# Gathering expert rows in four parts for VectorE's transposes, and a new order of the first products

## The chip, the cores and the metric

The kernel runs on one core of one Trainium2 chip. The metric is device time in microseconds, of which the median over several executions is given. TensorE is called PE here (its weight loads PEld), VectorE DVE, ScalarE ACT, GpSimd POOL and the engine that issues most transfers SP.

## What is computed

One image of 256 channels and 48 x 48 = 2304 tokens passes through two layers, all in float32. Layer 0 normalises groups of channels, and adds attention over all tokens and four heads. Layer 1 adds an attention through 64 slices, and then a mixture of experts, which is the stage that the change is mostly about:

```python
x = x + _L0_conv_ref(_gn(x), ...)          # _gn: mean and variance over 32 groups of 8 channels
t = _to_tokens(x)                          # 2304 tokens of 256
t = t + _L1_attn_ref(_ln_t(t), ...)
...
gate_logits = xf @ Wg + bg                 # xf = _ln_t(t), 8 experts
top_w, top_i = jax.lax.top_k(gate_logits, 2)
top_w = jax.nn.softmax(top_w, axis=-1)
for e in range(8):
    h = gelu(xf @ W1[e] + b1[e])           # 256 -> 1024
    out = out + w_dense[:, e:e+1] * (h @ W2[e] + b2[e])
t = t + out
```

## The kernel before

**Front.** SP loads x in four pieces and then the weights Wq, Wk, Wv, Wo. `transposed` (L249) turns a 256 x 256 weight by four PE transposes into a PSUM tile `pw` of a ring of two, which ACT copies out. DVE reduces x to mean and variance of each channel (`mv`). A product of PE with `gmat` spreads the means over groups (`pg`, L275), DVE forms `dm`, a second product spreads the variances (`pg2`, L286), and DVE and POOL make `rstd` of it. Then DVE normalises x into `xn` (kept in `t_sb`), block by block of 512 tokens, and PE multiplies by Wq and Wk (L312, L316) and later Wv. A transpose of `brow` gives the biases as columns. `busy_first` (L263) adds a product whose result nobody reads. The engines' instructions are in most places kept in program order by `InOrder`, so that their line in the profile is that of the helper, L60.

**Gating** (from L1035). After the attention and the slices, DVE finds two experts for each token and a place for each of the 4608 choices in slots of 128 rows, each slot of one expert. There are 43 slots at most (`NSL`); 36 (`SURE`) are in use at least, and three more (`near`) are prepared. PE's products end in `pw`: for each row of a slot its token and weight. DVE turns that into `slot_t` (token, int32) and `slot_w`. Rows that no token fills point to one of 128 empty rows behind the 2304. `busy(n, spin)` runs n idle products of 256 columns. The normalised tokens lie in DRAM as `tn_d`, and the sum is kept in DRAM as `t_d`.

**Expert tiles** (from L1296). For each slot s:

- `rows` (L1226): one indirect DMA, issued by POOL, gathers 128 rows of 1 KB from `tn_d` into `xs`, a ring of two tiles.
- `load_w1` (L1234): SP loads the expert's W1, 1 MB, into a ring of two. W2 of all experts is already in SBUF.
- `turn` (L1241): PE transposes the two halves of `xs` into PSUM (`pt`), DVE copies them to `xT`.
- `first` (L1250): 16 products into `ph`, and ACT's gelu into `hid`.
- `second` (L1268): 8 products into `py` and DVE's bias and weight, into `y`. Behind the third product a function `meanwhile` is called, in which the turn of another slot stands.
- `scatter` (L1288): an indirect DMA of POOL adds the rows of `y` to `t_d`.

Each "product" in float32 is two matmul instructions in the profile. The main loop (L1348) is written so that iteration s issues `first(s)`, then the gather of slot s+2 and its W1 load, then `second(s-1)` with the turn of slot s+1 in it, then `scatter(s-1)`. Indirect DMAs are kept in written order on POOL (`issued`), so the gather of s+2 stands behind the scatter of s-2 and before that of s-1. A scatter waits until the one before has landed.

At s == 4, `judge` tests the ranges of the first attention's sums; it has a transpose `pm`. The rows of the last slot, 35, are not scattered: PE adds them at the end by a product with `here`, a 0/1 matrix of 128 rows by 2304 tokens. It is made from an iota of POOL (at s == 6) and comparisons of DVE with `held` (L1366, L1369). At the end `t_d` is read back, transposed by PE and written out.

Of the kernel before, what the change touches and what calls it, by code (L numbers as in the profile page):

```python
# [9 lines left out]
FP = mybir.dt.float32  # L10
AF = mybir.ActivationFunctionType
ALU = mybir.AluOpType
AX = mybir.AxisListType
PSUM = bass.MemoryType.PSUM

P = 128
C = 256
NT = 2304
NTT = NT // P
# [17 lines left out]
NSL = (2 * NT - E) // P + E  # L37
# [9 lines left out]
def bc(ap, shape):  # L47

    return ap.unsqueeze(2).to_broadcast(shape)
# [16 lines left out]
def layers(  # L66
# [69 lines left out]
    )  # L136

    stats = const.tile([P, NTT, 2], FP, name="stats")
    rstd_t = const.tile([P, NTT], FP, name="rstd_t")
# [81 lines left out]
    def rsqrt(dst, var, eps, n):  # L221

        ve = small.tile([P, n], FP, name="ve", tag="ve")
        dve.tensor_scalar(ve, var, eps, None, ALU.add)
        nc.gpsimd.tensor_tensor(dst, ve, mhalf[:, 0:n], ALU.pow)
# [18 lines left out]
    with proj, tc.tile_pool(name="ps_pj", bufs=5, space=PSUM) as ps_pj, tc.tile_pool(  # L244
        name="ps_spun", bufs=1, space=PSUM
    ) as ps_spun, tc.tile_pool(
        name="ps_w", bufs=2, space=PSUM
    ) as ps_w:
        def transposed(dst, raw):  # L249
            pw = ps_w.tile([P, 2, C], FP, name="pw", tag="pw")  # L250
            for ci in range(2):
                for co in range(2):
                    pe.transpose(
                        pw[:, ci, co * P : (co + 1) * P], raw[:, co, ci * P : (ci + 1) * P], ident
                    )
            nc.scalar.copy(dst, pw)
            return dst

        WqT = transposed(pj.tile([P, 2, C], FP, name="WqT"), raws["Wq"])
        WkT = transposed(pj.tile([P, 2, C], FP, name="WkT"), raws["Wk"])  # L260
        spun = ps_spun.tile([P, 256], FP, name="spun")

        def busy_first(n):  # L263
            for _ in range(n):
                pe.matmul(spun, ident, raws["Wq"][:, 0, :], start=True, stop=True)


# [6 lines left out]
        gm = gmat.rearrange("p a b -> p (a b)")  # L274
        pg = ps_w.tile([P, 512], FP, name="pw", tag="pw")  # L275
        pe.matmul(pg[:, 0:2], gm, mv[:, :, 0], start=True, stop=True)
        busy_first(1)
        dm = pj.tile([P, 2], FP, name="dm")
        dve.tensor_sub(dm, mv[:, :, 0], pg[:, 0:2])
        for c in range(2):  # L280
# [3 lines left out]
        mean = pj.tile([P, 2], FP, name="mean")  # L284
        dve.tensor_copy(mean, pg[:, 0:2])
        pg2 = ps_w.tile([P, 512], FP, name="pw", tag="pw")  # L286
        pe.matmul(pg2[:, 0:2], gm, dm, start=True, stop=True)
        rstd = pj.tile([P, 2], FP, name="rstd")
        rsqrt(rstd, pg2[:, 0:2], 1e-5, 2)
        xn = t_flat[:, 0 : 2 * NT].rearrange("p (c n) -> p c n", c=2)  # L290
        pb = ps_w.tile([P, 512], FP, name="pw", tag="pw")
        pe.transpose(pb[:, 0:78], brow, ident[0:78, 0:78])
        dve.tensor_copy(bcol, pb[:, 0:78])
        bq8 = pj.tile([P, 2], FP, name="bq8")
        dve.tensor_scalar(bq8, bcol[:, B_Q : B_Q + 2], 0.125, None, ALU.mult)
        WvT = transposed(pj.tile([P, 2, C], FP, name="WvT"), raws["Wv"])
        transposed(WoT, raws["Wo"])


        for bi, (t0, tn) in enumerate(TBLOCKS):  # L300
# [34 lines left out]
            if bi == 0:  # L335
                later_constants()

        def slice_weights():
# [71 lines left out]
    def busy(n, bank):  # L410

        for _ in range(n):
            pe.matmul(bank[:, 0:256], ident, Wqkv_sb[:, 0, 0:256], start=True, stop=True)
# [422 lines left out]
    gp = gating.enter_context(tc.tile_pool(name="gate", bufs=1))  # L836
    norm = gating.enter_context(tc.tile_pool(name="norm", bufs=2))


# [194 lines left out]
    slot_w = route.tile([P, NSL], FP, name="slot_w")  # L1034
    slot_t = route.tile([P, NSL], mybir.dt.int32, name="slot_t")  # L1035
    b1_e = bcol[:, 0 : E * NHC].rearrange("p (e f) -> p e f", e=E)
    b2_e = b2_bc.rearrange("p (e d) -> p e d", e=E)
    with gating, tc.tile_pool(name="onehot", bufs=1) as oh, tc.tile_pool(
# [113 lines left out]
        for n in (3, 6, 6, 3, 6, 6, 3, 3):  # L1152
# [22 lines left out]
            k += n  # L1175
        busy(11, spin)

        empties = gp.tile([P, NSL], FP, name="empties")
        dve.tensor_scalar(empties, pw[:, 0, :], 0.0, spare, ALU.is_equal, ALU.mult)
        dve.scalar_tensor_tensor(empties, pw[:, 0, :], -1.0, empties, ALU.add, ALU.add)  # L1180
        dve.tensor_scalar(slot_t, empties, 0.0, float(NT + P - 1), ALU.max, ALU.min)
        dve.tensor_copy(slot_w, pw[:, 1, :])

    def expert_of(s, engine):
# [6 lines left out]
    with tc.tile_pool(name="ps_h", bufs=1, space=PSUM) as ps_h, tc.tile_pool(  # L1191
# [17 lines left out]
        here = fin.tile([P, NT], FP, name="here")  # L1209
        held = fin.tile([P, 1], FP, name="held")  # L1210
        obs = cycle([fin.tile([P, 2, 512], FP, name=f"ob{k}") for k in range(3)])
# [14 lines left out]
        def rows(s, xs):  # L1226
# [5 lines left out]
            return xs  # L1232

        def load_w1(s, w1):  # L1234
            e = expert_of(s, mybir.EngineType.SP)
            nc.sync.dma_start(
                out=w1, in_=W1[bass.ds(e, 1)].rearrange("e (c p) f -> p (e c) f", p=P)
            )
            return w1

        def turn(xs):  # L1241

            pt = next(ring_pt)
            for c in range(2):
                pe.transpose(pt[:, c, :], xs[:, c * P : (c + 1) * P], ident)
            xT = next(ring_xT)
            dve.tensor_copy(xT, pt)
            return xT

# [50 lines left out]
        for s in range(2):  # L1300
            w1[SURE + s] = load_w1(SURE + s, next(ring_w1))
            xs[s] = rows(s, next(ring_xs))
        used = nc.values_load(
# [12 lines left out]
        def turn_next(s):  # L1316
            if s in xs:
                xT[s] = turn(xs.pop(s))

# [28 lines left out]
        for s in range(SURE):  # L1348
            hid[s] = first(s, xT.pop(s), w1.pop(s))
            if s + 2 < SURE:  # L1350
                xs[s + 2], w1[s + 2] = rows(s + 2, next(ring_xs)), load_w1(s + 2, next(ring_w1))
            if s == 0:
                turn_next(1)
            elif s < SURE - 2:
                scatter(s - 1, second(s - 1, hid.pop(s - 1), lambda: turn_next(s + 1)))
            if SURE - 3 <= s < SURE - 1:

                scatter(s, second(s, hid.pop(s), lambda: turn_next(s + 1) if s == SURE - 2 else None))
            if s == 4 and bad is not None:
                judge()  # L1360
            if s == 6:
                pool.iota(
                    here, pattern=[[1, NT]], base=0, channel_multiplier=0,
                    allow_small_or_imprecise_dtypes=True,
                )
                dve.tensor_copy(held, slot_t[:, SURE - 1 : SURE])  # L1366
            if 8 <= s < 8 + len(TBLOCKS):
                t0, n = TBLOCKS[s - 8]
                dve.tensor_scalar(here[:, t0 : t0 + n], here[:, t0 : t0 + n], held, None, ALU.is_equal)  # L1369

# [95 lines left out]
```

## Time and profile before

| | us |
|---|---|
| median of 3 runs | 1587.24 |
| lowest and highest | 1586.57, 1590.79 |
| the profiled execution | 1588.82 |
| its span, first to last instruction | 1587.1 |
| PE busy in it | 1559.0 (98%) |
| DVE, ACT, POOL busy | 1034.2, 830.7, 192.7 |
| transposes pt of slots' rows on PE | 72 matmuls of 0.273 |
| gathers xs on POOL | 36 of 1.08 |
| scatters on POOL | 38 of 1.58 |

The profile is that of one execution. A group of it is named by line, engine and operation, then output<-inputs, their size, and how often (x). In a timeline each row has its start, its duration, and in brackets how long the engine sat idle before it and who ended that. Matmuls overlap, so the time of one is read from the distance of starts. "issue" is idle time in which the engine waited for nothing that the profile shows.

### The profile page before, as it was taken

How to read it: one execution, taken by the hardware profiler on the slowest of the kernel's cores; microseconds unless marked ns; L12 is line 12 of the kernel's file. 1: busy time of each engine (PE TensorE's matmuls, PEld its weight loads, DVE VectorE, ACT ScalarE, POOL GpSimd, SP SyncE). 2: the span in 40 equal slices, each digit the busy share in tenths (PEclk: the TensorE clock that was granted, in tenths of full speed). 3: DMA queues.
4: the chain of work that ended last, by engine and by line, in shares of the span. 5: the costliest groups of instructions: out<-in, count | busy, mean ns of one | idle time of the engine just before them, and what ended most of it. 6: DMA issues, size and time to landing. Idle time of an engine off the chain costs nothing. (4 is left out here: it accounts for less than half of the span.)

```text
span 1587.1 us, 32093 instructions
## 1 busy us (share of the span) xinstructions
PE 1559.0 (98%) x13117; PEld 776.2 (49%) x13117; DVE 1034.2 (65%) x1291; ACT 830.7 (52%) x1167; POOL 192.7 (12%) x133
## 2 busy tenths in 40 slices
PE   7999999999999999999999999999999999999998
PEld 3633343333333333333333333333334689999996
DVE  6578787787777778878778778787787721111111
ACT  3256565555666556556556566566554533323231
POOL 0001001011010010110101101101010123433331
PEclk9999999999999999999999999999999999999999
DMA  4000000000000000000000000000000956666665
GB/s 136 1 1 1 1 1 3 6 1 1 9 1 1 8 1 2 7 2 2 4 5 2 2 8 1 1 8 1 1 2 28 331 161 193 175 190 174 192 171 161
DMA packets 55981, 79.30 MB, mean 50 GB/s; under 512 B 21471, under 2 KB 42158, under 8 KB 55694
## 3 DMA queue, kind: packets, MB, share of 16 engines
q1 hardware_dynamic: 47826, 66.45, 13.0%
q0 software_dynamic: 7344, 10.10, 3.8%
q8 instruction: 108, 1.77, 0.5%
q10 hardware_dynamic: 652, 0.56, 0.1%
q14 instruction: 51, 0.42, 0.1%
HBM read 62.94 MB, written 12.32 MB: 47 GB/s over the span
## 5 line engine op out<-in xcount | busy, mean ns | idle before, releaser
L60 ACT ACTIVATE p<-s 128x1024 f32<-128x1024 f32 x648 | 663.3, 1024 | 470.4 <-PE s L60 465.2
L60 DVE TENSOR_TENSOR acc<-acc,p 128x1024 f32<-128x1024 f32 x612 | 749.5, 1225 | 243.3 <-ACT p L60 237.5
L60 PE MATMUL av<-p,v_sb 64*64 64x512 f32 x5184 | 675.7, 590 | 3.1 <-ACT p L60 1.9
L60 PE MATMUL s<-q,kk 64*64 64x512 f32 x5184 | 674.7, 589 | 0.5 <-DVE tn L60 0.5
L60 PEld LDWEIGHTS s<-q,kk 64*64 64x64 f32 x5184 | 202.1, 133 | 353.6 <-issue 181.5
L60 PEld LDWEIGHTS av<-p,v_sb 64*64 64x64 f32 x5184 | 195.7, 131 | 358.5 <-ACT p L60 201.6
L60 ACT ACTIVATE hid<-ph,bcol 128x128 f32<-128x128 f32 x312 | 89.5, 368 | 199.9 <-PE ph L60 199.1
L60 POOL PARTITION_ALL_REDUCE total<-both x17 | 71.2, 4186 | 1012.6 <-ACT p L60 893.9
L60 PE MATMUL py<-w_sb,hid 128*128 x624 | 146.9, 379 | 0.0
L60 PEld LDWEIGHTS ph<-xT,w 128*128 128x128 f32 x1248 | 145.3, 192 | 2.7 <-issue 0.8
L60 PE MATMUL ph<-xT,w 128*128 128x128 f32 x1248 | 145.7, 275 | 0.6 <-issue 0.6
L60 DVE COPY xT<-pt 128x256 f32<-128x256 f32 x39 | 16.5, 425 | 161.0 <-PE pt L60 161.0
L60 PEld LDWEIGHTS py<-w_sb,hid 128*128 128x128 f32 x624 | 112.9, 190 | 12.3
L1217 POOL DMA_INDIRECT t_d<-y,slot_t x38 | 60.1, 1581 | 163.2 <-DVE y L60 145.4
L60 DVE TENSOR_TENSOR y<-py,b_bc 128x256 f32<-128x256 f32 x39 | 16.6, 425 | 77.4 <-PE py L60 77.4
L1217 POOL DMA_INDIRECT xs<-tn_d,slot_t x36 | 38.8, 1078 | 15.9 <-issue 10.1
L60 DVE RECIPROCAL rinv<-rinv 128x256 f32<-128x256 f32 x17 | 29.7, 1746 | 0.0
L60 DVE TENSOR_TENSOR acc<-p 128x1024 f32<-128x1024 f32 x18 | 22.1, 1226 | 4.9 <-ACT p L60 3.3
L329 DVE TENSOR_SCALAR q<-pp,bcol 64x512 f32<-64x512 f32 (+1 forms) x30 | 20.8, 694 | 6.7 <-PE pp L312 6.4
L60 DVE TENSOR_REDUCE up<-av 128x512 f32<-128x1024 f32 x17 | 20.8, 1225 | 5.0 <-PE av L60 5.0
L60 POOL TENSOR_TENSOR rstd_t<-ve,mhalf 128x2 f32<-128x2 f32 (+2 forms) x13 | 11.1, 850 | 103.2 <-DVE ve L60 95.7
L60 PE MATMUL spin<-Wqkv_sb,ident 128*128 128x256 f32 x84 | 19.4, 381 | 0.0
(295 smaller groups left out, 590.6 us busy)
## 6 DMA issues: line engine op xcount, KB each, us to landing
w<-in_L_ffn_W_dram SPq DMA_DIRECT2D x39, 1024.0 KB, 5.9
w_sb<-in_L_ffn_W_dram SPq DMA_DIRECT2D x8, 1024.0 KB, 11.8
t_sb<-turned SPq DMA_DIRECT2D x224, 8.0 KB, 1.8
x_sb<-in_x_dram SPq DMA_DIRECT2D x3, 576.0 KB, 4.9
t_d<-t_sb SPq DMA_DIRECT2D x2, 768.0 KB, 10.2
tn_d<-tn SPq DMA_DIRECT2D x2, 768.0 KB, 5.7
t_sb<-t_d SPq DMA_DIRECT2D x3, 512.0 KB, 4.1
out_dram<-ob SPq DMA_DIRECT2D x3, 512.0 KB, 3.0
```

The costliest lines, as they stand in the source:

```text
L60: return self.tc.keep_in_program_order(getattr(self.engine, name)(*args, **kwargs))
L329: nc.vector.tensor_scalar(dst, pq[rows, 0:tn], bcol[rows, B_Q + m : B_Q + m + 1], 0.125, ALU.add, ALU.mult,)
L1217: new = nc.gpsimd.indirect_dma_start(**kwargs)
```

## The change

In the front, the means' product moves ahead of Wk's transposes, and the variances' product and the biases' transpose stand between the first two and the last two of them. The three results get a PSUM bank of their own (`pgb`). `busy_first` goes. Wo's transposes move behind the first block of q and k products.

For 26 of the slots (`in_parts`: s from 2 to 35 but those with s % 4 == 1), the gather is split in four. `part_t` holds for each slot and part k the index of a 256-byte quarter row: partition 32q + s gets quarter q of the token of row 32k + s. So each 32 x 32 block that DVE transposes by itself already lies where its transpose belongs, and two DVE transposes from `xs` to `xT` take the place of PE's two and the copy. `quad` (made by ACT), `quarter`, four products and one DVE step make `part_t` in the gating, and the 11 idle products there become 4 and 5. Channels are now dealt to partitions in pairs (2p + c instead of 128c + p), in W1's load and in both kinds of turn.

For the last slot, `here` is made by DVE alone from `steps` and `held`, which now has a column for each block of 128 tokens; POOL's iota goes.

```diff
+    quarter = const.tile([P, 1], FP, name="quarter")
+    for q in range(4):
+        nc.vector.memset(quarter[q * 32 : (q + 1) * 32, :], float(q))
     stats = const.tile([P, NTT, 2], FP, name="stats")
...
     with proj, tc.tile_pool(name="ps_pj", bufs=5, space=PSUM) as ps_pj, tc.tile_pool(
-        name="ps_spun", bufs=1, space=PSUM
-    ) as ps_spun, tc.tile_pool(
+        name="ps_g", bufs=1, space=PSUM
+    ) as ps_g, tc.tile_pool(
         name="ps_w", bufs=2, space=PSUM
     ) as ps_w:
-        def transposed(dst, raw):
+        def transposed(dst, raw, meanwhile=lambda: None):
             pw = ps_w.tile([P, 2, C], FP, name="pw", tag="pw")
             for ci in range(2):
                 for co in range(2):
                     pe.transpose(
                         pw[:, ci, co * P : (co + 1) * P], raw[:, co, ci * P : (ci + 1) * P], ident
                     )
+                if ci == 0:
+                    meanwhile()
             nc.scalar.copy(dst, pw)
             return dst
         WqT = transposed(pj.tile([P, 2, C], FP, name="WqT"), raws["Wq"])
-        WkT = transposed(pj.tile([P, 2, C], FP, name="WkT"), raws["Wk"])
-        spun = ps_spun.tile([P, 256], FP, name="spun")
-        def busy_first(n):
-            for _ in range(n):
-                pe.matmul(spun, ident, raws["Wq"][:, 0, :], start=True, stop=True)
+        pgb = ps_g.tile([P, 96], FP, name="pgb")
+        pg = pgb[:, 0:4].rearrange("p (a b) -> p a b", a=2)
+        pb = pgb[:, 16:94]
...
         gm = gmat.rearrange("p a b -> p (a b)")
-        pg = ps_w.tile([P, 512], FP, name="pw", tag="pw")
-        pe.matmul(pg[:, 0:2], gm, mv[:, :, 0], start=True, stop=True)
-        busy_first(1)
+        pe.matmul(pg[:, 0, :], gm, mv[:, :, 0], start=True, stop=True)
         dm = pj.tile([P, 2], FP, name="dm")
-        dve.tensor_sub(dm, mv[:, :, 0], pg[:, 0:2])
+        dve.tensor_sub(dm, mv[:, :, 0], pg[:, 0, :])
         for c in range(2):
             dve.scalar_tensor_tensor(
                 dm[:, c : c + 1], dm[:, c : c + 1], dm[:, c : c + 1], mv[:, c, 1:2], ALU.mult, ALU.add
             )
         mean = pj.tile([P, 2], FP, name="mean")
-        dve.tensor_copy(mean, pg[:, 0:2])
-        pg2 = ps_w.tile([P, 512], FP, name="pw", tag="pw")
-        pe.matmul(pg2[:, 0:2], gm, dm, start=True, stop=True)
+        dve.tensor_copy(mean, pg[:, 0, :])
+        def spread():
+            pe.matmul(pg[:, 1, :], gm, dm, start=True, stop=True)
+            pe.transpose(pb, brow, ident[0:78, 0:78])
+        WkT = transposed(pj.tile([P, 2, C], FP, name="WkT"), raws["Wk"], spread)
         rstd = pj.tile([P, 2], FP, name="rstd")
-        rsqrt(rstd, pg2[:, 0:2], 1e-5, 2)
+        rsqrt(rstd, pg[:, 1, :], 1e-5, 2)
         xn = t_flat[:, 0 : 2 * NT].rearrange("p (c n) -> p c n", c=2)
-        pb = ps_w.tile([P, 512], FP, name="pw", tag="pw")
-        pe.transpose(pb[:, 0:78], brow, ident[0:78, 0:78])
-        dve.tensor_copy(bcol, pb[:, 0:78])
+        dve.tensor_copy(bcol, pb)
         bq8 = pj.tile([P, 2], FP, name="bq8")
         dve.tensor_scalar(bq8, bcol[:, B_Q : B_Q + 2], 0.125, None, ALU.mult)
         WvT = transposed(pj.tile([P, 2, C], FP, name="WvT"), raws["Wv"])
-        transposed(WoT, raws["Wo"])
...
                 later_constants()
+                transposed(WoT, raws["Wo"])
...
     norm = gating.enter_context(tc.tile_pool(name="norm", bufs=2))
+    quad = gp.tile([P, 4, 4, 32], FP, name="quad")
+    act.copy(quad, ident.rearrange("p (k s) -> p k s", k=4).unsqueeze(2).to_broadcast([P, 4, 4, 32]))
...
     slot_t = route.tile([P, NSL], mybir.dt.int32, name="slot_t")
+    part_t = route.tile([P, 4, NSL], mybir.dt.int32, name="part_t")
     b1_e = bcol[:, 0 : E * NHC].rearrange("p (e f) -> p e f", e=E)
...
             k += n
-        busy(11, spin)
-        empties = gp.tile([P, NSL], FP, name="empties")
+        busy(4, spin)
+        empties = route.tile([P, NSL], FP, name="empties")
         dve.tensor_scalar(empties, pw[:, 0, :], 0.0, spare, ALU.is_equal, ALU.mult)
         dve.scalar_tensor_tensor(empties, pw[:, 0, :], -1.0, empties, ALU.add, ALU.add)
         dve.tensor_scalar(slot_t, empties, 0.0, float(NT + P - 1), ALU.max, ALU.min)
+        dve.tensor_scalar(empties, empties, 0.0, float(NT + P - 1), ALU.max, ALU.min)
         dve.tensor_copy(slot_w, pw[:, 1, :])
+        pq = ps_lg.tile([P, 4, NSL], FP, name="pq")
+        for k in range(4):
+            pe.matmul(
+                pq[:, k, :], quad[:, k, :, :].rearrange("p q s -> p (q s)"), empties, start=True, stop=True,
+            )
+        dve.tensor_scalar(part_t, pq, 4.0, quarter, ALU.mult, ALU.add)
+        busy(5, spin)
...
         here = fin.tile([P, NT], FP, name="here")
-        held = fin.tile([P, 1], FP, name="held")
+        held = fin.tile([P, NTT], FP, name="held")
         obs = cycle([fin.tile([P, 2, 512], FP, name=f"ob{k}") for k in range(3)])
...
+        def in_parts(s):
+            return 2 <= s < SURE and s % 4 != 1
+        def parts(s, xs):
+            if not in_parts(s):
+                return rows(s, xs)
+            for k in range(4):
+                indirect(
+                    out=xs[:, k * 64 : (k + 1) * 64], out_offset=None,
+                    in_=tn_d.rearrange("t (q d) -> (t q) d", q=4),
+                    in_offset=bass.IndirectOffsetOnAxis(ap=part_t[:, k, s : s + 1], axis=0),
+                    bounds_check=4 * (NT + P) - 1, oob_is_err=True,
+                )
+            return xs
         def load_w1(s, w1):
             e = expert_of(s, mybir.EngineType.SP)
             nc.sync.dma_start(
-                out=w1, in_=W1[bass.ds(e, 1)].rearrange("e (c p) f -> p (e c) f", p=P)
+                out=w1, in_=W1[bass.ds(e, 1)].rearrange("e (p c) f -> p (e c) f", p=P)
             )
...
             for c in range(2):
-                pe.transpose(pt[:, c, :], xs[:, c * P : (c + 1) * P], ident)
+                pe.transpose(pt[:, c, :], xs.rearrange("p (d c) -> p c d", c=2)[:, c], ident)
             xT = next(ring_xT)
             dve.tensor_copy(xT, pt)
+            return xT
+        def turn_parts(xs):
+            xT = next(ring_xT)
+            for c in range(2):
+                dve.transpose(
+                    xT[:, c, :].rearrange("p (k s) -> p k s", k=4),
+                    xs.rearrange("p (k r c) -> p c k r", k=4, c=2)[:, c],
+                )
             return xT
...
             w1[SURE + s] = load_w1(SURE + s, next(ring_w1))
-            xs[s] = rows(s, next(ring_xs))
+            xs[s] = parts(s, next(ring_xs))
         used = nc.values_load(
...
             if s in xs:
-                xT[s] = turn(xs.pop(s))
+                xT[s] = (turn_parts if in_parts(s) else turn)(xs.pop(s))
...
             if s + 2 < SURE:
-                xs[s + 2], w1[s + 2] = rows(s + 2, next(ring_xs)), load_w1(s + 2, next(ring_w1))
+                xs[s + 2], w1[s + 2] = parts(s + 2, next(ring_xs)), load_w1(s + 2, next(ring_w1))
             if s == 0:
...
             if s == 6:
-                pool.iota(
-                    here, pattern=[[1, NT]], base=0, channel_multiplier=0,
-                    allow_small_or_imprecise_dtypes=True,
-                )
-                dve.tensor_copy(held, slot_t[:, SURE - 1 : SURE])
+                dve.tensor_scalar(
+                    held, lim[:, 0:NTT], -1.0, empties[:, SURE - 1 : SURE], ALU.mult, ALU.add
+                )
             if 8 <= s < 8 + len(TBLOCKS):
                 t0, n = TBLOCKS[s - 8]
-                dve.tensor_scalar(here[:, t0 : t0 + n], here[:, t0 : t0 + n], held, None, ALU.is_equal)
+                shape = [P, n // P, P]
+                dve.tensor_tensor(
+                    here[:, t0 : t0 + n].rearrange("p (k r) -> p k r", r=P),
+                    steps.unsqueeze(1).to_broadcast(shape),
+                    bc(held[:, t0 // P : (t0 + n) // P], shape), ALU.is_equal,
+                )
```

## Prediction

> **What bounds the kernel.** I read the busy shares first: PE is busy 98% of the 1587.1 us span, and in the slices it is at 9 or more tenths everywhere but the first and the last. So an edit is worth what it takes off PE's stream, or off a place where PE waits. The change touches three places: the first 20 us, the gating near 1277 us, and the expert tiles, 1283 to 1565 us. The windows of the tile stage carry the argument (columns: span; busy us and count of PE, PEld, DVE, ACT, POOL; granted clock; DMA share; GB/s).
>
> ```profile
> core 0: us, PE busy (x) PEld busy (x) DVE busy (x) ACT busy (x) POOL busy (x), PEclk, DMA share, GB/s
> 1404.54:1433.53 28.99, 28.99 (x202) 27.14 (x202) 4.81 (x12) 9.25 (x32) 10.66 (x8) 1.00 0.67 180
> ```
>
> Four tiles take 28.99 us, 7.25 each, and PE is never idle in them: these tiles are PE, nothing else. DVE and ACT have room; POOL is busy 2.67 us per tile and DMA 67% of 7.25 us. The timeline shows the period of one tile, from ph to the next ph (start, us, engine, operation, [idle before]):
>
> ```profile
> 1534.83 3.73 PE L60 MATMUL ph<-xT,w 128*128 128x128 f32 x32
> ...
> 1536.12 1.58 POOL L1217 DMA_INDIRECT t_d<-y,slot_t  x1 [4.28 <-DVE y L60]
> ...
> 1538.01 1.08 POOL L1217 DMA_INDIRECT xs<-tn_d,slot_t  x1 [0.30 <-issue]
> ...
> 1539.70 0.38 PE L60 MATMUL pt<-ident,xs 128*128 128x128 f32 x2
> ...
> 1542.08 3.73 PE L60 MATMUL ph<-xT,w 128*128 128x128 f32 x32
> ...
> 1543.37 1.58 POOL L1217 DMA_INDIRECT t_d<-y,slot_t  x1 [4.28 <-DVE y L60]
> ```
>
> and, by luck, one tile that turns nothing between two ph:
>
> ```profile
> 1298.75 3.73 PE L60 MATMUL ph<-xT,w 128*128 128x128 f32 x32
> ...
> 1302.32 3.62 PE L60 MATMUL py<-w_sb,hid 128*128 x16
> ...
> 1305.78 3.73 PE L60 MATMUL ph<-xT,w 128*128 128x128 f32 x32
> ```
>
> 1298.75 to 1305.78 is 7.03 us; with the two transposes it is 7.25. So a pair of transposes costs PE 0.22 us.
>
> **Tiles turned by VectorE.** in_parts holds for s = 2 to 35 without 5, 9, ..., 33: 34 - 8 = 26 tiles. Each drops two transposes from PE: 26 x 0.22 = **-5.7 us**, if all that is added stays beside PE. What is added, per such tile:
>
> DVE: a 0.42 us copy goes, two transposes of 128x128 come. The nearest row is STREAM_TRANSPOSE turned<-x_sb, 128x256, 0.44 us; half the elements with a step of two lie between 0.22 and 0.44 each. I take 0.3, so 0.6 per tile against DVE's 6 us of idle. The transposes wait for four gathers instead of for PE, and behind them in DVE's order stands y of the tile before; that y is due only when PE has ended its py, so only a late gather costs anything. The `here` and `held` edits stay on DVE too and take the 2.63 us iota off POOL.
>
> POOL: three gathers more. A gather occupies POOL 1.08 us and is followed by 0.30 ("issue"); a scatter 1.58 and 0.30. Per tile in parts: 1.88 + 4 x 1.38 = 7.40 us, just above the new 7.03; per tile in one piece 1.88 + 1.38 = 3.26. In each group of four, 3 x 7.40 + 3.26 = 25.5 us against PE's 3 x 7.03 + 7.25 = 28.3. POOL is 90% full, runs late by 0.37 us per tile in parts, 1.1 us by the third, and makes it good on the fourth. Bounds: the gather may cost 1.01 us as the ungrouped ones at 1281.88 did (7.12 per tile) or 1.58 as a scatter of as many rows does. The count of rows per DMA stays 128, so I take 1.08.
>
> Is the last part in time? Counting from the start of ph of tile s, the gather for s+2 starts at 1538.01 - 1534.83 = 3.2 us, the fourth part at 3.2 + 3 x 1.38 = 7.3. A gather lands a median 5.4 us after its issue (2.7 to 6.6), so at 12.7, 13.8 with the lateness, and the turn is done at 14.4 at worst. ph of s+2 starts at 2 x 7.03 = 14.06. But 5.4 us is for a gather that runs beside the 1 MB load of w1, issued at about 3.7 and landed 5.9 later, at 9.6; the fourth part outlives it. The gathers that ran beside less landed in 3.0 us (median of xs around 1280 us): 7.3 + 1.1 + 3.0 + 0.6 = 12.0. I take no wait, with 0.3 us in every third tile as the other end (8 groups, +2.4 us).
>
> DMA engines: 128 pieces of 1 KB become 512 of 256 B. [...] The rows leave it wide open. From 1340 to 1540 us the software queue's 5328 packets took 21.7% of 16 engines x 200 us, 130 ns each, beside w1; at that price 512 pieces are 512 x 130 / 16 = 4.2 us where 0.8 was spent, and DMA would need 4.9 - 0.8 + 4.2 = 8.3 us of 7.03. But the 17920 packets of about 103 B from DVE's earlier transposes took 1.2% of 16 x 1040 us, 11 ns each: 0.4 us per tile. By bytes (28.42 MB of the hardware queue in 43.3% of 16 x 200 us is 20.5 B/ns) 128 KB is 0.4 us[...]. [...] I take the small price: DMA stays near 70%, and costs nothing. w1 is now read as 8 KB rows instead of 4 KB ones[...].
>
> [...]
>
> Tiles in one piece: the transposes now read xs with a step of two. No row has a stationary operand of that kind. A weight load could stay at 0.14 us or double: 0 to 0.14 x 2 x 13 tiles = 3.6 us. I take +0.3.
>
> **Judging.** `pm`, half of a turn, and a pause are inserted near 1340 us: ph starts at 1331.31 (the tile before), 1340.55 and 1346.39, 15.08 us where two tiles take 14.50. In the new order four py, not three, stand ahead of pm, and the half turn that waited for its gather is gone: **-0.3 us** (0 to 0.5).
>
> **Gating.** 11 spins at 0.44 us become 9, and four small products with `quad` come. Spins ended at 1282.0, and the first turn waited 0.99 us for PE's sequencer behind them, while its gather (issued 1278.88, landing 3.5 us) was there at 1282.4. So PE may start 0.4 us earlier at most: **-0.2**. slot_t stays ahead of the added DVE steps, and part_t is ready near 1280 while the first part is wanted at 1289.8. There four gathers stand ahead of a scatter due at 1292.80 and push it to about 1295.3; its next user comes at 1300.04, after the 3.8 us of landing. The `quad` copy of 128x512 (0.59 us as WqT's) falls into ACT's idle 5.65 us before 1236.18.
>
> **The front.**
>
> ```profile
> 11.75 1.11 PE L60 MATMUL pw<-ident,Wk_raw 128*128 128x128 f32 x4 [0.27 <-DMA Wk_raw<-in_L_conv_Wk_dram]
> ...
> 12.65 0.43 PE L60 MATMUL pw<-mv,gmat 128*128 128x2 f32 x2
> ...
> 15.42 0.55 DVE L303 TENSOR_SCALAR t_sb<-x_sb,mean,rstd 128x512 f32<-128x512 f32 x1 [0.54 <-POOL rstd L225]
> ...
> 16.38 2.84 PE L312 MATMUL pp<-t_sb,WqT 128*128 128x512 f32 x4
> ...
> 20.77 1.88 PE L312 MATMUL pp<-t_sb,WqT 128*128 128x512 f32 x4
> ```
>
> The mean's product waits behind Wk's transposes, which wait for Wk; mv was ready at 11.08 (10.76 + 0.32), Wq's transposes end at 11.48. It can start 1.17 us earlier, the variance's some 1.3 (it also waited for WkT's copy to free pw), and xn 1.3 earlier, near 14.1. With Wo's transposes gone from the way, the first q product starts near 14.95 instead of 16.38, 1.4 us. But the first weight loads are 0.85 us apart up to 18.09 and 0.43 from 18.63 on: PE is at half pace until about 18.35, though the granted clock reads 1.00. [...] If the doubling moves with the work, 1.4. Against it stand Wo's four transposes, now among products at full pace: 4 x 0.11 = 0.4. Ends: -1.0[...]. [...]**-0.3**.
>
> **Sum.** -5.7 + 0.3 - 0.3 - 0.2 - 0.3 = -6.2 us. The profiled execution took 1588.82 (span 1587.1 and 1.7 around it): 1582.6. It stands 1.6 above the median of the runs, 1587.24; from the median I get **1581.0**. Own range 1578 to 1583.5.
>
> **Rivals.**
> (a) Gathers late: some tiles of each group wait for the last part, 0.3 to 0.7 us in 8 groups, +2.4 to +5.6: 1583.4 to 1586.6, middle 1585. For it: POOL at 90% and a last part with 2 us to spare at best. Against: one tile in four repairs it.
> (b) Slower: the gather queue takes PE's place as the bound. At the scatter's 1.88 us per DMA, POOL needs 4 x 1.88 + 13 x 1.88 = 32.0 us per four tiles against 29.0 before: +3.0 x 8.5 groups = +25, 1612. With 130 ns per packet instead, (3 x 8.3 + 4.9) / 4 = 7.4 us per tile, +0.15 x 34 = +5, 1592. It is slower than before once a gather and its pause pass (28.99 - 7.52) / 13 = 1.65 us. Against: rows per DMA don't change.
> (c) The change does not do what it says: the freed time is taken by the w1 load. Freed 3.6 us after ph starts, landed by 7.4 at most, it is due at 14.06. Then 1587.
>
> Chances: forecast 0.70, (a) 0.18, (b) 0.09, (c) 0.03. A measurement here tells about 0.3%, 4.8 us, from no change. The forecast clears that by 1.4 us and part of its range doesn't; (a) mostly counts as same: faster 0.71, same 0.19, slower 0.10. Range 1577 to 1586.5: the forecast with the front's better end and most of (a).
>
> **What would show it.** Windows of four tiles: 28.3 us with PE without idle, and no pt matmuls in three of four. POOL: gathers at 1.08 us and a share near 90%; 1.5 and more means (b). DVE's transposes waiting for DMA xs and PE idle before ph means (a). xn at 14.1 and the first q product near 15 show the front; its pace shows whether the doubling moved. I am wrong if PE is idle in the tiles, or if the turns with a step of two load slower.

## The result, and the profile after

| | before | after |
|---|---|---|
| median of 12 runs, us | 1588.28 | 1584.26 |
| lowest to highest, us | 1586.57 to 1590.79 | 1583.55 to 1589.47 |
| profiled execution, us | 1588.82 | 1584.24 |
| its span, us | 1587.1 | 1582.4 |

The ratio of the medians is 0.9978, with a 95% interval of 0.9969 to 0.9987, or 2.1 to 4.9 us: 4.0 us faster in the medians, where 6.2 had been forecast. The sign held, and the mechanism in the tiles. (The runs of before shown first had a median of 1587.24; 12 of them have 1588.28.) About 2 us are missing, and the spans, 4.7 us apart, tell where.

**The tiles gave what was forecast.** Four tiles in three stretches of the changed kernel's windows (columns as before: span; PE, PEld, DVE, ACT, POOL busy; clock; DMA share; GB/s):

```profile
1354.34:1382.67 28.33, 28.33 (x196) 26.68 (x196) 6.63 (x18) 9.16 (x32) 19.83 (x17) 1.00 0.65 186
1411.01:1439.35 28.34, 28.34 (x196) 26.69 (x196) 5.08 (x15) 9.14 (x32) 19.97 (x18) 1.00 0.66 182
1496.02:1524.35 28.33, 28.33 (x196) 26.68 (x196) 5.08 (x15) 9.15 (x32) 19.88 (x18) 1.00 0.66 188
```

28.33 us where four tiles took 28.99, PE never idle, POOL busy 19.9. One tile with a turn and one without, in the timeline:

```profile
1502.88 3.73 PE L60 MATMUL ph<-xT,w 128*128 128x128 f32 x32
...
1506.07 1.05 POOL L1229 DMA_INDIRECT xs<-tn_d,part_t  x1 [0.30 <-issue]
...
1507.75 0.39 PE L60 MATMUL pt<-ident,xs 128*128 128x128 f32 x2
...
1510.14 3.73 PE L60 MATMUL ph<-xT,w 128*128 128x128 f32 x32
...
1512.68 0.51 DVE L60 STREAM_TRANSPOSE xT<-xs 128x128 f32<-128x128 f32 x2 [1.50 <-DMA xs<-tn_d,part_t]
...
1517.16 1.05 PE L60 MATMUL ph<-xT,w 128*128 128x128 f32 x8
```

The distances of ph are 7.26 and 7.02 us. DVE's two transposes overlap to 0.51 us and have waited for the last part, but end at 1513.19, four us before the ph at 1517.16 that needs them. From the first tile's py to the last tile's ph the stage took 272.42 us before (1287.61 to 1560.03) and 266.32 after (1289.66 to 1555.98): -6.1.

**The gating gave two microseconds away.** The timeline of before between the last product of the gating and the first tile (PEq is PE's sequencer):

```profile
1277.05 4.95 PE L60 MATMUL spin<-Wqkv_sb,ident 128*128 128x256 f32 x22
1282.99 0.41 PE L60 MATMUL pt<-ident,near_xs 128*128 128x128 f32 x2 [0.99 <-PEq L1308]
1283.96 3.81 PE L60 MATMUL ph<-xT,w 128*128 128x128 f32 x32 [0.56 <-issue]
1287.61 1.46 PE L60 MATMUL py<-w_sb,hid 128*128 x6
```

and of after:

```profile
1276.92 1.93 PE L60 MATMUL spin<-Wqkv_sb,ident 128*128 128x256 f32 x8
1278.69 0.98 PE L60 MATMUL pq<-empties,quad 128*128 128x43 f32 x8
1279.50 2.40 PE L60 MATMUL spin<-Wqkv_sb,ident 128*128 128x256 f32 x10
1283.35 0.47 PE L60 MATMUL pt<-ident,near_xs 128*128 128x128 f32 x2 [1.45 <-PEq L1347]
1284.39 5.44 PE L60 MATMUL ph<-xT,w 128*128 128x128 f32 x32 [0.56 <-issue]
...
1289.66 1.46 PE L60 MATMUL py<-w_sb,hid 128*128 x6
```

From the first idle product to the first py it was 10.56 us, and is 12.74: pt starts 0.5 us later, and the first tile's ph takes 5.44 us instead of 3.81. The windows of after say why the same 32 matmuls take longer:

```profile
1281.90:1285.28 3.38, 1.37 (x11) 1.24 (x11) 0.42 (x1) 0.00 (x0) 2.77 (x3) 1.00 0.39 113
1285.28:1288.65 3.37, 3.37 (x19) 3.37 (x18) 0.00 (x0) 1.14 (x4) 0.14 (x1) 0.50 0.15 47
1288.65:1290.00 1.35, 1.35 (x12) 1.32 (x12) 0.00 (x0) 0.07 (x1) 0.00 (x0) 1.00 0.00 0
```

The last column but two is the granted clock. For 3.4 us it is 0.50, and the 3.4 us before it held only 1.37 us of PE work.

**The rest.** The attention ends 0.2 us earlier (last av at 1216.20, before 1216.42), of which 0.13 is left at the first idle product. From the last slot's ph to the end it is 26.42 us instead of 27.07; over the profiles of all runs below this stretch takes 26.2 to 28.8 us, and 27.2 in e4, which makes `here` as the changed kernel does, so the 0.65 us are not shown to come from the change. Sum: -0.13 + 2.18 - 6.10 - 0.65 = -4.7.

### The profile page after: what moved, and what is told of

The parts are those of the page before. It is cut to its first block, busy times and chain, and to the rows that moved or that the text cites. A ratio compares the mean times of both kernels' runs of the same rounds, so it can differ in the third digit from the quotient of the medians.

```text
span 1582.4 us, 32230 instructions
## 1 busy us (share of the span) xinstructions
PE 1553.9 (98%) x13067; PEld 773.7 (49%) x13067; DVE 1038.5 (66%) x1323; ACT 831.0 (53%) x1168; POOL 270.4 (17%) x210
## 5 line engine op out<-in xcount | busy, mean ns | idle before, releaser
L60 PE MATMUL py<-w_sb,hid 128*128 x624 | 142.8, 379 | 0.0
L1229 POOL DMA_INDIRECT xs<-tn_d,part_t x104 | 106.5, 1024 | 37.9 <-issue 30.5
L60 DVE STREAM_TRANSPOSE xT<-xs 128x128 f32<-128x128 f32 x52 | 13.1, 291 | 55.7 <-DMA xs<-tn_d,part_t 55.7
L60 DVE COPY xT<-pt 128x256 f32<-128x256 f32 x13 | 5.4, 424 | 51.8 <-PE pt L60 51.8
```

The lines of the kernel that those rows point to most:

```text
L60: return self.tc.keep_in_program_order(getattr(self.engine, name)(*args, **kwargs))
L1229: new = nc.gpsimd.indirect_dma_start(**kwargs)
```

## Experiments

Theories. A: the missing 2 us are lost in the gating, by its new order of PE's work. B: the half clock only depends on where a window of the clock falls, with any order. C: the loss is in tiles or front. Two more, D and E, came up on the way. All differences are to the kernel before as run with each, and "first idle product" is the first spin behind the products pw.

### pq behind nine idle products, and more idle products

e1_pq_last:

```diff
-        busy(4, spin)
+        busy(9, spin)
...
         dve.tensor_scalar(part_t, pq, 4.0, quarter, ALU.mult, ALU.add)
-        busy(5, spin)
```

> The changed kernel with the gating's idle products in one run again: nine of them, and the four products pq behind them instead of between four and five. All else as changed. Theory A (the missing gain was lost in the gating, because pq waits for DVE in the middle of the idle products, which holds PE's sequencer back and leaves a clock window with too little PE work): the first pt starts about 0.4 us earlier than in the changed kernel, ph of the first tile takes 3.8 us instead of 5.44 at a granted clock of 1.00, and the median falls by 1.6 to 2.1 us, to about 1582.3. Theory B (the half clock is a matter of where the clock's windows happen to fall in an execution, not of the order): ph is at half clock in some executions of either kernel, and the median stays at 1584.3 or moves by less than 1 us. Theory C (the loss is not in the gating but in the tiles or the front): ph may be back to 3.8, but the time stays at 1584.3.

e2_eight_behind:

```diff
-        busy(5, spin)
+        busy(8, spin)
```

> The changed kernel with eight idle products behind pq instead of five, so that PE is busy up to about 1283.2 us. Theory A: the pause of 1.45 us before the first pt is filled up to a few tenths, ph is back to 3.8 us at clock 1.00, and the median falls by about 1.4, to 1582.9, if the sequencer's work for the branch runs beside the idle products. If the sequencer begins that work only when the last idle product is out, pt starts 1.3 us later and the gain of 1.6 is nearly all lost: 1584.0. Theory B: as the changed kernel or 1.3 slower. Theory C: no faster than the changed kernel.

Both were slower than every theory had it: 1596.08 (1591.85 to 1602.12) and 1594.79 us (1589.31 to 1603.74), against 1588.42. In the profile of e1 the gating is no better: pt starts 6.87 us after the first idle product, later than in the changed kernel, and ph again takes 5.44. In e2 ph is back to 3.81, but pt starts 7.67 us after. The three idle products more delay pt by 1.2 us. But the large loss is elsewhere. PE's weight loads in the timeline of e1, among the tiles:

```profile
1414.19 0.52 PEld L60 LDWEIGHTS ph<-xT,w 128*128 128x128 f32 x3
1414.95 0.19 PEld L60 LDWEIGHTS ph<-xT,w 128*128 128x128 f32 x1 [0.24 <-issue]
1415.67 0.19 PEld L60 LDWEIGHTS ph<-xT,w 128*128 128x128 f32 x1 [0.54 <-issue]
1416.39 0.41 PEld L60 LDWEIGHTS ph<-xT,w 128*128 128x128 f32 x3 [0.53 <-issue]
1417.13 0.19 PEld L60 LDWEIGHTS ph<-xT,w 128*128 128x128 f32 x1 [0.33 <-issue]
1417.84 1.36 PEld L60 LDWEIGHTS ph<-xT,w 128*128 128x128 f32 x6 [0.53 <-issue]
```

In the middle of a product whose operands are all there, PE goes on only every 0.72 us, and the profile names nothing that it waits for. The tile stages of the two profiled executions are 9.6 and 10.0 us longer than after's; in e1 a window at half clock (1417.5 to 1420.9) behind such pauses is in it. What follows: these two runs say nothing on A in their medians, and there is a trouble in the tiles that the changed kernel's own profile doesn't show.

### The new gating alone, and the change without parts

e3_gating_alone is the kernel before with quad, quarter, part_t and pq between four and five idle products; nobody reads part_t.

> The kernel before with the new gating alone (quad, quarter, part_t, pq between four and five idle products); the rows are gathered and turned as before, and nobody reads part_t. Theory A: slower than before by 0.4 (pt later) to 2.1 us (ph at half clock too): 1588.5 to 1590. Theory B: by 0.4 at most in the median. Theory C: the same as before within 0.3 us.

1590.18 us against 1588.42, +1.8; ratio 1.0012, interval 1.0006 to 1.0019, that is 1.0 to 3.0 us. pt starts 6.56 us after the first idle product (before: 5.94), ph takes 5.34, the whole 12.70. A stands in the median too; B and C had 0.4 at most.

e4_one_piece:

```diff
         def in_parts(s):
-            return 2 <= s < SURE and s % 4 != 1
+            return False
```

> The changed kernel with no slot in parts: every slot is gathered in one piece and turned by PE, with the step of two. Front, gating and the layout of W1 as changed. If the tiles in parts are worth what was forecast (26 x 0.22 us less on PE), this is 5.7 us slower than the changed kernel, about 1590, and a tile takes 7.25 us. If the turn with a step of two costs its 0.056 us per weight load on PE's stream, a tile takes 7.25 + 0.11 = 7.36 and it is 5.7 + 26 x 0.11 = 8.6 us slower. If the tiles in parts give less than forecast (theory C), the difference is below 4 us.

1590.60 against 1588.42: 2.2 us slower than before. The change is 4.0 faster, so its parts are worth 6.2 us, against 5.7 forecast. (Each is a difference to runs of before taken with it, and uncertain by about 1 us.) Four of its tiles, each turned with the step of two:

```profile
1405.66:1434.68 29.02, 29.02 (x202) 27.39 (x200) 4.81 (x12) 9.12 (x32) 10.64 (x8) 1.00 0.63 183
```

29.02 against 28.99: a strided weight load lasts 0.196 us instead of 0.141, and PE's stream pays nothing for it.

### pq behind the first turn

f1_pq_after_turn, with `quad` in the pool of constants:

```diff
-        busy(4, spin)
+        busy(11, spin)
...
-        pq = ps_lg.tile([P, 4, NSL], FP, name="pq")
...
-        busy(5, spin)
...
         turn_next(SURE)
+        pq = next(ring_pt).rearrange("p a b -> p (a b)")[:, 0 : 4 * NSL].rearrange("p (k n) -> p k n", k=4)
+        for k in range(4):
+            pe.matmul(
+                pq[:, k, :], quad[:, k, :, :].rearrange("p q s -> p (q s)"), empties, start=True, stop=True,
+            )
+        dve.tensor_scalar(part_t, pq, 4.0, quarter, ALU.mult, ALU.add)
         hid[SURE] = first(SURE, xT.pop(SURE), w1.pop(SURE))
```

> The changed kernel with the eleven idle products of the kernel before, and the four products pq behind the first turn (pt) instead of among the idle products, where PE waits 0.56 us for xT anyway. Theory A (44 instructions of PE stand ahead of the branch as before instead of 52[...], and PE's pauses in a clock window shrink from 2.0 to about 1.0 us, too little for the half clock): the first pt starts 5.9 us after the first idle product instead of 6.4, pq costs 0.4 us on PE's path, ph takes 3.8 us at clock 1.00 in every execution, the median falls by 0.7 (as far as the half clock came in every second execution) to 1.6 us, to 1582.7 to 1583.6. Theory B (only where the clock's windows fall): no change of the median beyond 0.5 us. Theory D (what slowed the two kernels with another number of idle products, PE standing without an instruction for 0.2 to 1 us at a time among the tiles, is set by where PE's code lies and can come with any edit): 1590 and more, with pauses of PE put down to issue between 1300 and 1560 us.

Its timeline (pq is in a tile of the ring pt, and so carries that name):

```profile
1276.58 4.95 PE L60 MATMUL spin<-Wqkv_sb,ident 128*128 128x256 f32 x22
1282.45 0.48 PE L60 MATMUL pt<-ident,near_xs 128*128 128x128 f32 x2 [0.92 <-PEq L1340]
1282.77 0.98 PE L60 MATMUL pt<-empties,quad 128*128 128x43 f32 x8
1283.58 3.82 PE L60 MATMUL ph<-xT,w 128*128 128x128 f32 x32
1287.23 1.46 PE L60 MATMUL py<-w_sb,hid 128*128 x6
```

10.65 us to py, as in the kernel before (10.56): the four products fill the wait for xT, and the half clock is gone. The median, 1589.50 (1585.76 to 1592.16), is spoilt by the same pauses of PE: its tile stage took 274.0 us, 7.7 more than after's.

f2_pq_after_turn_seven has seven idle products instead of the eleven.

> The same with seven idle products instead of eleven. [...]pt starts as early as its gather allows, some 0.5 us earlier than with eleven (5.4 us after the first idle product), but PE stands idle for about 2 us before it, and the half clock is back in some executions: about the time of the run with eleven, up to 1 us either way. If pt waits for the gather alone, it starts as with eleven.

pt starts 5.09 us after the first idle product, ended by its gather, and py comes after 9.87. The median, 1592.18, again has the pauses.

### What the pauses come with

e5_all_parts puts all 34 slots in parts (`return 2 <= s < SURE`).

> The changed kernel with all 34 slots from 2 to 35 in parts, none in one piece between them. If gathers and scatters on POOL stay beside PE (4 x 1.32 + 1.92 = 7.2 us per tile by the changed kernel's rows, against 7.03 of PE), POOL falls behind by 0.17 us per tile, 5 us over the stage, of which the two tiles of lead hide some 2: 8 x 0.22 = 1.8 us gained, about 3 lost, 1584 to 1587. If POOL becomes the bound with more per DMA than these rows show, 1590 or more. If POOL's time per part is less than that, 1582.5.

1606.08 us, 17 slower than before: PE is busy only 190.8 of 200 us in the tiles, full of such pauses. POOL is not what bounds it: in these 200 us it is busy 147.5 and waits 15 us for DVE's results. s1_one_idle_more has `busy(11, spin)` for `busy(10, spin)` ahead of the products pw (L1132):

> The changed kernel with one idle product more (eleven instead of ten) in the stretch before the products pw near 1265 us, where PE waits 1.04 us for ACT anyway. It moves nothing by itself and shifts PE's code behind it by one product's instructions. Theory D: PE stands without an instruction among the tiles again, 1590 and more. Otherwise the time stays at 1584.3 within 0.5 us, and the slow tiles of the two earlier kernels come from their own order in the gating.

One hidden product more, and the median is 1593.14, 9 us above the changed kernel. One of its six runs took 1586.94; that is the one profiled, with few pauses. So where the code lies seems to decide (D); or it decides only where the gathers stand dense (E). Four runs part the two.

> The kernel before with one idle product more near 1265 us, as s1 had it for the changed kernel. If the slow tiles come from where PE's code lies alone (theory D), this is slower than the kernel before by 4 us and more. If it takes the dense gathers in parts beside it (theory E[...]), it stays at 1588.5 within 0.5 us, without pauses of PE put down to issue.

> e4 (the changed kernel, every slot in one piece) with one idle product more near 1265 us: PE's code lies as in s1 up to the tiles. Theory E: as e4, 1590.6 within 0.7 us, no pauses put down to issue. Theory D: slower by 4 us and more.

The same line edited in the kernel before: 1587.90 against 1588.01, ratio 1.0000 (0.9993 to 1.0006). And in e4: 1590.61, e4 had 1590.60. Neither has a pause. Without parts the shift is worth nothing, so D falls.

> The changed kernel with two idle products more near 1265 us. Theories D and E: another place of the code, so anything between 1584 (the changed kernel's own place is an ordinary one) and 1595 (its place was a lucky one). If it is at 1584.3, the slow tiles of s1 are no matter of the place in general; with 1590 and more the changed kernel's 1584.3 is the exception among its neighbours.

1584.63 (1582.50 to 1590.12): with two products more, the profile has no pause, and by their times most of the other runs had few. 1584.3 is neither the rule nor an exception.

h1_every_second is f1 with fewer parts:

```diff
-            return 2 <= s < SURE and s % 4 != 1
+            return 2 <= s < SURE and s % 2 == 0
```

> f1 (pq behind the first turn, eleven idle products) with every second slot in parts instead of three of four: 17 tiles. POOL needs 7.2 + 3.2 us of two tiles' 14.28, 73% instead of 90%. Theory E, if the density of gathers is what matters: no or few pauses of PE, tiles of 7.03 and 7.25 in turn, 17 x 0.22 = 3.7 us less than one piece, with the end's 0.65 and the front's 0.2 about 1584. Theory D: 1588 and more, with pauses as in f1.

1583.67 (1583.16 to 1584.59) against 1588.01: 4.3 us faster, ratio 0.9970 (0.9958 to 0.9982). No pause in its profile; two tiles in parts and two in one piece make four tiles of

```profile
1439.35:1467.68 28.33, 28.33 (x197) 26.71 (x195) 5.00 (x14) 9.12 (x32) 16.48 (x15) 1.00 0.65 186
```

(a window cut for the other kernel's period: read POOL, 16.5 us busy instead of 20). h2_two_of_three takes `s % 3 != 1`.

> h1 with two of three slots in parts, 23 tiles instead of 17; POOL 83% full by the rows. If the pauses come with POOL's fill beyond some point between 73% and 90%: either 6 x 0.22 = 1.3 us faster than h1, 1582.4, or pauses and 1585 and more.

1592.81 (1590.69 to 1600.84), with pauses. Of the nine kernels with two thirds of the slots or more in parts, seven were slow, with pauses in their profiles, and two (the changed kernel and s2) not in most runs; the three with half (h1, g1, h3) and the five without parts (before, b1, e3, e4, e6) have no pause put down to issue. So E fits these runs: the pauses came only with many tiles in parts, and there a shift of code or order decided whether they came. That it is the density of the gathers is not shown: with it, these runs also changed the number of DVE's transposes, and from h1 to h2 there came to be two tiles in parts in a row. What PE waits for stays open too. As far as the trace shows, it is not a packet on the queue of instructions, which the next section reads: of the 69 pauses above 0.15 us that are put down to issue in e1, e2, e5, f1, f2 and h2, only two had one under way.

### The gating's price where nothing covers it

g1_gating_kept is the changed kernel with every second slot in parts, so h1 with the gating as changed.

> The changed kernel with every second slot in parts and nothing else: against h1 it has the gating as changed (pq between four and five idle products). With no pauses in the tiles this is the gating's price alone. Theory A: half clock for the first tile where the clock's window lies badly, and pt 0.5 us later: 1.1 (half clock in every second execution) to 2.1 us slower than h1, 1584.8 to 1585.8. Theory B (no matter of the order): as h1 within 0.4 us.

1586.34 against 1588.53: 2.2 us faster than before where h1 is 4.3 faster. The gating's order costs 2.1 us in the median, to be read with the intervals, 1.0 to 3.0 us faster for g1 and 2.9 to 6.7 for h1. Its profile again has the half clock (ph 5.38 us, py 12.92 us after the first idle product).

h3_seven is h1 with seven idle products.

> h1 with seven idle products instead of eleven. As in f2, pt comes 0.6 to 0.8 us earlier (5.1 us after the first idle product instead of 5.7 to 5.9), and PE stands for about 1.9 us before it: 1583.0 if the clock stays, up to 1 us more where a window of the clock holds that pause, so 1582.9 to 1584.2, not told apart from h1 if both come in turn.

1584.54 against 1588.53, 4.0 us faster; pt starts 5.18 us after the first idle product and py after 9.96, 0.5 less than in h1. Not told apart from h1, as expected.

## Why the forecast was right, and where it was wrong

The forecast of the tiles came true with its mechanism; the step that failed is the gating's, forecast at -0.2 us and measured at some +2.1. The prediction had set 4.8 us as the least that a measurement can tell here; the 4.0 measured stay below it, though their interval leaves out zero. The 1584.26 us lie outside the forecast's own range (1578 to 1583.5) and close to the middle of rival (a), 1585, but by chance: the late gathers of (a) didn't come.

- **Tiles, -5.7 us: right.** 6.1 in the trace, judging included, and 6.2 in the medians (e4). 0.22 us per turn, 28.3 us for four tiles and no wait of PE are as forecast.
- **DVE's transposes at 0.3: right,** 0.29.
- **POOL at 90%: nearly.** A gather in parts took 1.02 us instead of the 1.08 taken, and a scatter 1.62: busy 19.9 of 28.3 us, with 0.30 behind each of the 17 DMAs 25.0, 88%. The 25 gathers that ran beside a y x slot_w took 1.01 us, no more than the others in parts (1.03), and that operation 0.38 instead of 0.35 in the mean.
- **Small pieces cost DMA almost nothing: right.** Between 1340 and 1540 us the software queue went from 5328 packets in 21.7% to 7140 in 22.2% of the engines' time. That is 0.5% of 3200 us for 1812 packets, some 9 ns each, near the 11 ns of the row that was taken and far from 130; by it a tile in parts takes 0.05 us more of the DMA engines. W1's packets changed from 4 to 8 KB at the same time, so what each of the two did to the software queue's time can't be told apart here.
- **The turn with a step of two, +0.3: nothing** (e4: 29.02 us for four tiles against 28.99). The load is 0.055 us longer, but it runs beside the matmul before: in after's timeline pt's loads start at 1507.53, ahead of the end of py at 1507.91.
- **Judging, -0.3: right.** The two tiles around pm take 14.39 us, 0.11 over 7.03 + 7.25, where they took 15.08, 0.58 over 14.50: -0.5.
- **Front, -0.3: right in size,** -0.2. The -0.3 left the end of the half pace at 18.35 us, which was the author's estimate: 1.7 slow products of 0.43 are 0.7, less 0.4 for Wo's transposes. xn came 0.9 us earlier (14.55), not 1.3, since Wk landed 0.6 later. The first q product came 1.2 earlier. And half pace held to some 18.9 us (weight loads 0.85 us apart up to 18.72), where before's ended at 18.3: this execution's windows of the clock stood 0.6 us later, which at half pace is worth some 0.3 us. By this estimate the front would have given 0.5 with the windows in the same place, so the fit has chance in it.
- **The end:** 0.65 us less, not in the sum, and no more than the stretch differs from run to run.
- **Gating, -0.2: this is the step that failed.** It measured +2.2 in the profile, +1.8 alone (e3), and 2.1 between g1 and h1. The step counted idle products, 11 against 9. It saw the 0.99 us that pt waits for PE's sequencer, but took them to follow the end of those products, down to the landing of pt's gather, and so let PE start up to 0.4 us earlier; for the clock it had no term. Two things were missed.

First, pt waits neither for the gather (in before it had landed at 1282.36, 0.63 us ahead of pt) nor for the end of PE's products (4.95 us after the first idle product in before, 4.98 in after, 4.91 in e1). It comes at a fixed distance behind a packet on the queue of instructions. Behind the gating stand branches over the slots that may not be in use. In the DMA view, a packet of 16 KB on that queue starts at 1280.2 in before and at 1280.5 in after. Over the profiles, in us after the first idle product:

| kernel | PE instructions from first idle product to branch | packet starts | packet ends | pt |
|---|---|---|---|---|
| f1 | 44 | 2.7 | 4.0 | 5.87 |
| before | 44 | 3.1 | 4.1 | 5.94 |
| after | 52 | 3.6 | 4.6 | 6.43 |
| e1 | 52 | 3.6 | 5.0 | 6.87 |
| e2 | 64 | 4.9 | 5.8 | 7.67 |

(Counted are weight loads and matmuls.) In all fifteen profiles in which the trace has pt wait for PE's sequencer, pt starts 1.85 to 1.90 us behind the packet's end; e1's pt is 0.44 us later than after's, and its packet took 1.4 us instead of 1.0. Over all of them the packet starts at 2.7 to 3.1 us with 44 instructions and at 3.5 to 3.9 with 52. No view shows what the packet holds, nor why pt follows it. What the profiles show is the order: with more instructions ahead of the branch, packet and first tile came later, and only with few of them (28 in f2 and h3, pt at 5.09 and 5.18 us) was the gather what pt waited for.

Second, the clock. PE stood idle 1.45 + 0.56 = 2.0 us between 1281.9 and 1284.4, all in one window of 3.4 us, and the next window ran at half clock: 1.6 us. In before it stood 0.99 + 0.56 = 1.55 us and kept the clock, in e3 1.92 and lost it. In e4, with the changed gating, a border of the windows at 1282.6 cut the same idle time into 0.8 and 1.3, and ph took 3.81. But the amount of idle time in a window is no sharp limit, as windows of s1 (first two lines) and h1 show:

```profile
1281.09:1284.50 3.41, 1.60 (x9) 1.10 (x8) 0.00 (x0) 0.00 (x0) 2.73 (x3) 1.00 0.40 107
1284.50:1287.91 3.41, 2.85 (x24) 2.68 (x25) 0.42 (x1) 0.32 (x2) 1.32 (x2) 1.00 0.31 97
...
1225.28:1228.69 3.41, 1.85 (x14) 1.48 (x13) 1.90 (x8) 1.36 (x6) 0.00 (x0) 1.00 0.97 332
1228.70:1232.10 3.40, 3.22 (x12) 2.91 (x13) 2.06 (x7) 0.65 (x2) 0.00 (x0) 0.50 1.10 357
```

s1 stood idle 1.81 us and kept the clock, h1 1.56 and lost it. Over the seventeen profiles, and leaving out the last 15 us, windows with 1.92 us and more of idle PE lost the clock each time (six windows); between 1.55 and 1.85 six lost it and six kept it; below that it was lost once, among the pauses of f2. What decides in between stays open. h1's loss near 1230, in a stretch of PE's work that no edit touches, came in five of the seventeen profiles (b1, e2, e5, h1, s1) and cost 1.1 us there: from the end of the attention to the first idle product they take 60.7 to 60.9 us, the others 59.5 to 59.9.

So B has a share. With the changed order, the half clock was in five of eight profiles (after, e3, s2, e6, g1, but not e4, e5, s1), and in e1 but not e2; with eleven or seven idle products in one run and pq behind the branch or absent it was in none of seven (before, b1, f1, f2, h1, h2, h3). The prediction had weighed PE's pace in the front, and did not ask the same of the pause in the gating.

Of the rivals, (a) fails: DVE's transposes waited 55.7 us in all for the gathers, and PE never for them. (c) fails: w1 landed a median 6.8 us after its issue where it took 5.9 (0.9 us more, for which the prediction had set nothing), and PE waited for none. (b) is wrong for this change, but its sign came true one step further, in e5, though not by the price per gather: that stayed at 1.03 us, and the loss sits in PE's pauses. The sum behind (b)'s 1592 has a slip: 128 packets at 130 ns on 16 engines are 1.04 us, not 0.8. With that a tile in parts needs 8.0 us of DMA, the mean of four tiles is 7.2, and that is no slower than before's 7.25.

The fastest version here is h1: the gating mended by pq behind the first turn, and half the slots in parts. Its 4.3 us are not separable from the change's 4.0 by their intervals, but none of its six runs lay outside 1583.2 to 1584.6. The two gains together, after's 26 tiles and the mended gating (f1), did not add up, because of the pauses.

## What to carry to other kernels

Ahead of a branch, count PE's instructions: here the first tile behind it came 0.5 us later and more with eight more of them, so move work that nobody needs at once to the far side, into a wait that is there anyway. Of every pause of PE ask how much of a 3.4 us window it takes together with its neighbours, not only how long it is; 2.0 us in one window cost 1.6 more here, and between 1.55 and 1.85 us it could go either way. And if a kernel's time jumps by several us with an edit that PE hides, as s1's did by 9, look for pauses put down to issue before believing any median.

## What was not expected of the hardware

- In after and before the clock's changes fit one grid of windows through the execution. In after the clock falls at 1285.25 and, at the end, at 1582.21: 296.96 us, or 87 steps of 3.4133 us. 371 such steps back from the first lies 18.9, and there the front's weight loads change their distance from 0.85 to 0.43 us (18.72 to 19.24). In before the fall at 1585.02 leads 459 steps back to 18.3, where its front did the same (18.09 to 18.63). The grid's place differs from execution to execution (17.0 to 20.2 us in the seventeen profiles). If the end of the half pace goes with it in all of them, as it does in these two, then as an estimate from these figures half of the difference, up to 1.6 us, is scatter in the time of one and the same kernel from this alone.
- Behind a branch PE's first instruction kept a fixed distance to a packet on the queue of instructions: 1.85 to 1.90 us behind its end, in all fifteen profiles in which it waited for PE's sequencer, whether the packet took 0.95 or 1.41 us. What fills the 1.85 us is not shown.
- PE's pauses of 0.72 us among the tiles, with nothing to wait for in the profile, came only with two thirds of the slots or more in parts, and a shift of code by one product could bring them or not: 5 to 12 us in the median of the kernels with three of four slots in parts that had them.
